# A layer norm's 1/std: a power on GpSimd, or a logarithm and an exponential on ScalarE

## The chip, the cores and the metric

The kernel runs on one core of a Trainium2 chip. A core has five engines with a queue each: TensorE (PE, matmuls; its weight loads are listed as PEld), VectorE (DVE), ScalarE (ACT), GpSimd (POOL) and SyncE (SP), which here issues the DMAs. Each engine works through its own queue in order and waits on semaphores for the others. The metric is the device time of one execution in microseconds.

## The reference

The input is 32 images of 128 channels and 56 x 56 pixels, in float32. Four layers follow one another, each of the form x = x + f(groupnorm(x)):

- layer 0: a 1x1 convolution with weights mixed by attention, then three dilated depthwise 3x3 convolutions with SiLU, summed
- layer 1: a cubic B-spline, the same for every element
- layer 2: linear attention over pooled cells, then a depthwise 3x3 convolution
- layer 3: a Mamba layer over the 3136 pixels as a sequence. It begins with a layer norm over the 128 channels of each pixel, and this is where the change lies:

```python
mu = jnp.mean(xs, axis=-1, keepdims=True)
var = jnp.mean(jnp.square(xs - mu), axis=-1, keepdims=True)
xn = (xs - mu) * lax.rsqrt(var + 1e-05) * norm_w + norm_b
...
delta = jax.nn.softplus(jnp.einsum('blr,dr->bld', dt, dt_proj_w) + dt_proj_b)
dA = jnp.exp(delta[..., None] * A)
...
h = dA_t * h + dBu_t
y = jnp.einsum('bdn,bn->bd', h, C_t)
```

The scan over pixels has 256 inner channels and 16 states each.

## The kernel before, in words

**Tiling.** The 128 channels lie on the 128 partitions. An image is cut into 7 chunks of 8 rows, that is 448 columns (`CH`). The 16 states of a chunk are handled two at a time for each half of the inner channels, in 16 steps (`STEPS`); so there are 32 x 7 = 224 chunks and 3584 steps.

**A step of the scan** (class `Scan`): ACT makes the decay exp(delta A) (`decay`, tile `da`, two instructions of 448 columns, in PSUM). DVE multiplies `du` by B into `h` and runs two scans over it (`state`); `h` has three buffers. POOL multiplies `h` by C into `hc`, which has two buffers (`products`). PE sums `hc` into `y` (`add`).

**The inputs of a chunk's scan** (`ssm_inputs`): matmuls from the normed `xn` give `xc`, `dbl` and the raw step sizes. The softplus is max(v,0) + ln(1 + exp(-|v|)): DVE takes the maximum into `delta`, ACT takes the absolute value, the exponential and the logarithm into `du`. POOL adds the two into `delta` and multiplies by `xc` into `du`; SP then moves both into the layout of the scan, with 16 DMAs a chunk. In the same stage the layer norm of the chunk after next is computed.

**The layer norm** (`layer_norm`, line 964): one matmul subtracts the channel mean (and applies the group norm) in PSUM, ACT takes the square and a copy `cen`, and a matmul with 1/128 gives the variance in PSUM. ACT then takes ln(var + eps) and exp(-0.5 times it) into `rstd`; POOL multiplies `cen` by `rstd` and applies weight and bias into `xn`. Ln and the kernel's other ACT functions (Exp, Tanh) are in different activation tables, so a Ln has an `ACT_TABLE_LOAD` ahead of it and another behind. For this the Ln of the softplus is passed in as `other` and kept together with the variance's Ln (lines 980 to 983). The first layer norm of an image is called from `until_scan` (line 1154), without `other`; after the last chunk (`norm is None`) only the softplus's Ln is left.

**The order of the work.** While one image is scanned, layers 1 and 2 of the next image (`until_scan`) and layer 0 of the one after (`first_layer`) are interleaved. In each group of images the instructions are collected by `Plan` with a price for each (`price`, line 163) and a due time that comes back from the work depending on it, and then put out in a planned order (`order`, `issue`, line 338, which is why nearly all instructions have line 338 in the profile). `together` keeps calls as one unit of this plan. On GpSimd the plan prices a two-input operation of over 8 columns at 0.14 + 0.00212 us a column, whatever it computes, and a power of up to 8 columns at 0.52 us. Six images make one turn of the loop (`UNROLL`), five turns, with two images ahead in the pipeline and two left over.

The group norms (`group_stats`, line 600) already take their 1/std, one column wide, by a power on GpSimd:

```python
nc.gpsimd.tensor_tensor(rs[:], ve[:], mhalf[:], ALU.pow)
```

`mhalf`, `one` and `lneps` (lines 446 to 448) are columns holding -0.5, 1 and 1e-5.

Of the kernel before, what the change touches and what calls it, by code (L numbers as in the profile page):

```python
# [14 lines left out]
AF = mybir.ActivationFunctionType  # L15
ALU = mybir.AluOpType
AX = mybir.AxisListType

P = 128
# [3 lines left out]
CH = ROWS * W  # L23
NCH = L // CH
# [338 lines left out]
def tile_conv_stack(ctx: ExitStack, tc: tile.TileContext, out: bass.AP, x: bass.AP, w: dict):  # L363
    nc = tc.nc
    B = x.shape[0]

    plan = Plan(nc, tc)
# [73 lines left out]
    def column(name, value):  # L441
        t = const.tile([P, 1], F32, name=name)
        nc.vector.memset(t[:], value)
        return t

    mhalf = column("mhalf", -0.5)
    one = column("one", 1.0)
    lneps = column("lneps", LN_EPS)
# [105 lines left out]
    xns = [const.tile([P, CH + DCONV - 1], F32, name=f"xn{k}") for k in range(3)]  # L554
# [6 lines left out]
    du = const.tile([P, DI, CH], F32, name="du")  # L561
# [18 lines left out]
    nc = plan  # L580

    def psum(cols=CH, rows=P):
        t = ps_mm.tile([P, 512], F32, tag="mm", name="mm")
        return t[:rows, :cols]
# [35 lines left out]
    def silu(dst, ps):  # L620

        t = tmp.tile([P, CH], F32, tag="v", name="t")
        nc.scalar.activation(t[:], ps, AF.Tanh)
        nc.vector.scalar_tensor_tensor(dst, t[:], 1.0, ps, ALU.add, ALU.mult)
# [332 lines left out]
    def norm_weights(st, ctr, cb):  # L957
# [3 lines left out]
        pm = psum(1)  # L961
        nc.tensor.matmul(pm, ctr[:], mg[:], start=True, stop=True)
        nc.vector.tensor_scalar_mul(cb[:], pm, -1.0)
    def layer_norm(xt, xn, j, norm, before=None, other=None):


        if norm is None:
            nc.scalar.activation(other, other, AF.Ln, bias=one[:, 0:1])
            return
        ctr, cb = norm  # L970
        pm = psum()
        nc.tensor.matmul(pm, ctr[:], xt[:, j * CH : (j + 1) * CH], start=True, stop=True)
        sq = tmp.tile([P, CH], F32, tag="v", name="sq")
        nc.scalar.activation(sq[:], pm, AF.Square, bias=cb[:, 0:1])
        cen = tmp.tile([P, CH], F32, tag="v", name="cen")
        nc.scalar.activation(cen[:], pm, AF.Identity, bias=cb[:, 0:1])
        pv = psum()
        nc.tensor.matmul(pv, jmat[:], sq[:], start=True, stop=True)
        rstd = tmp.tile([P, CH], F32, tag="v", name="rstd")
        with plan.together():  # L980
            nc.scalar.activation(rstd[:], pv, AF.Ln, bias=lneps[:, 0:1])
            if other is not None:
                nc.scalar.activation(other, other, AF.Ln, bias=one[:, 0:1])
        nc.scalar.activation(rstd[:], rstd[:], AF.Exp, scale=-0.5)
        nc.gpsimd.tensor_mul(rstd[:], cen[:], rstd[:])
        if before is None:
            nc.gpsimd.memset(xn[:, : DCONV - 1], 0.0)
        else:
            nc.gpsimd.tensor_copy(xn[:, : DCONV - 1], before[:, CH:])
        nc.gpsimd.tensor_scalar(xn[:, DCONV - 1 :], rstd[:], normw[:, 0:1], normb[:, 0:1], ALU.mult, ALU.add)  # L990
# [11 lines left out]
    def ssm_inputs(xt, k, norm):  # L1002

        dbl, xc = dbls[k % 2], xcs[k % 2]
        j, xn = k % NCH, xns[k % 3]
        for db in range(DI):
            ch = slice(db * P, (db + 1) * P)
            ps = psum()
            for i in range(DCONV):
                nc.tensor.matmul(ps, winT[:, i, ch], xn[:, i : i + CH], start=(i == 0), stop=False)  # L1010
            nc.tensor.matmul(ps, cbT[:, ch], onesr[:].to_broadcast([P, CH]), start=False, stop=True)
            silu(xc[:, db, :], ps)
            yield 3.3
        ps = psum()
        for db in range(DI):
            nc.tensor.matmul(ps, xprojT[:, db, :], xc[:, db, :], start=(db == 0), stop=(db == DI - 1))
        nc.scalar.copy(dbl[:], ps)
        nc.vector.scalar_tensor_tensor(dbl[:], dbl[:], low[:, 0:1], ps, ALU.mult, ALU.add)
        yield 1.7

        for db in range(DI):
            ps = psum()
            nc.tensor.matmul(ps, dtT[:, db * P : (db + 1) * P], dbl[:], start=True, stop=True)
            nc.scalar.activation(du[:, db, :], ps, AF.Abs, bias=dtb[:, db : db + 1])
            nc.vector.tensor_scalar(delta[:, db, :], ps, dtb[:, db : db + 1], 0.0, ALU.add, ALU.max)
            yield 0.8
        nc.scalar.activation(du[:], du[:], AF.Exp, scale=-1.0)
        layer_norm(xt, xns[(k + 1) % 3], j + 1, norm if j + 1 < NCH else None, xn, du[:])
        nc.gpsimd.tensor_add(delta[:], delta[:], du[:])
        nc.gpsimd.tensor_mul(du[:], delta[:], xc[:])  # L1030
        yield 4.0

        for db in range(DI):
            for src, dst in zip((delta, du), halves):
                dst = dst[DI * (k % 2) + db]
                for s in range(2):
                    for r in range(2):
                        nc.sync.dma_start(dst[Q * s : Q * s + Q, r, :], src[Q * r : Q * r + Q, db, :])
        yield 1.0
# [106 lines left out]
    def until_scan(b):  # L1146

        xt = xts[b % 3]
        st = yield from spline(xt, sts[b % 2])
        st = yield from linear_attention(xt, st)  # L1150
        norm = carried[b % 2]
        norm_weights(st, *norm)
        yield 5.0
        layer_norm(xt, xns[b * NCH % 3], 0, norm)
        yield 5.0

    def first_inputs(b):
        return ssm_inputs(xts[b % 3], b * NCH, carried[b % 2])
# [37 lines left out]
    def images(first, count, ahead):  # L1196
# [18 lines left out]
        for b in range(count):  # L1215
# [5 lines left out]
            for j in range(NCH):  # L1221
# [10 lines left out]
                if j + 1 < NCH:  # L1232
                    following = ssm_inputs(xt, k + 1, carried[b % 2])
                elif more:
                    following = first_inputs(b + 1)
# [153 lines left out]
```

## Time and profile before

| | |
|---|---|
| median of 3 runs | 16330.96 us (16321.42 to 16344.79) |
| profiled execution | 16316.11 us |
| its span | 16314.3 us, 212520 instructions |
| mean granted TensorE clock | 0.893 |
| each of 224 layer norms: logarithm, exponential | 634 ns and 568 ns |
| HBM traffic over the span | 59 GB/s |

The profile is of one execution. The span runs from the first to the last instruction. In a line for a group of instructions stand the line of code, the engine, the operation, the tile written and the tiles read, their shapes and the count; then the busy time in us and the mean of one in ns; then how long the engine had stood idle just ahead of these instructions, and what released it. In the table of waits a line reads: who waited, for whom, total us, times, longest us. In the order in time a line gives start, duration and, in brackets, the idle time ahead of it and its releaser.

### The profile page before, as it was taken

The numbers are of one execution on the slowest core, as the hardware profiler recorded it, in microseconds if no ns is written. First come the engines' busy times: TensorE is split into PE (matmuls) and PEld (weight loads), VectorE is DVE, ScalarE is ACT, GpSimd is POOL, SyncE is SP. The second block draws the span as 40 slices with busy tenths as digits, with TensorE's granted clock in tenths as the row PEclk, the third lists the DMA queues.
The fourth block names the chain that finished last, engine by engine and source line by source line (L and its number), as shares of the span: only waits on it lengthen the run. The fifth ranks groups of instructions, "written<-read, shape, count | busy, mean of one in ns | idle before, by whom it ended". The sixth has DMA issues, their size and how long they took to land. (4 is left out here: it accounts for less than half of the span.)

```text
span 16314.3 us, 212520 instructions
## 1 busy us (share of the span) xinstructions
PE 14202.3 (87%) x66400; PEld 4559.9 (28%) x66400; DVE 14306.2 (88%) x17314; ACT 11713.4 (72%) x21127; POOL 10785.0 (66%) x6406
## 2 busy tenths in 40 slices
PE   6888898888898888988888888888888898888887
PEld 2222222222222222222222222222222222222222
DVE  2898988989889898899988888888898898888889
ACT  3777777777677776777776777767777677776675
POOL 2676666666666666667666666666676666766666
PEclk7888998889998898998989988899988899888888
DMA  6344444344443444434444434444344444344421
GB/s 143 93 101 98 98 112 96 89 99 101 106 104 88 100 97 101 109 94 94 101 99 107 102 86 98 99 105 107 91 98 97 100 108 106 85 97 99 101 56 34
DMA packets 986159, 1589.93 MB, mean 97 GB/s; under 512 B 175622, under 2 KB 611209, under 8 KB 984331
## 3 DMA queue, kind: packets, MB, share of 16 engines
q1 hardware_dynamic: 985002, 1576.06, 41.0%
q8 instruction: 538, 8.81, 0.2%
q14 instruction: 619, 5.06, 0.1%
HBM read 785.62 MB, written 173.18 MB: 59 GB/s over the span
## 5 line engine op out<-in xcount | busy, mean ns | idle before, releaser
L338 POOL TENSOR_TENSOR hc<-h,cb 128x896 f32<-128x896 f32 x3584 | 7476.1, 2092 | 4173.5 <-DVE h L338 2178.7
L338 DVE TENSOR_TENSOR_SCAN h<-da,last,h 128x448 f32<-128x448 f32 x6144 | 6772.7, 1135 | 498.2 <-ACT da L338 451.3
L338 ACT ACTIVATE da<-delta,alog 128x448 f32<-128x448 f32 x7168 | 4481.8, 633 | 2635.3 <-DVE h L338 2369.4
L338 PE MATMUL y<-hc,sums 128*64 128x448 f32 x14336 | 3997.9, 638 | 625.6 <-POOL hc L338 617.8
L338 DVE TENSOR_TENSOR h<-du,pb 128x896 f32<-128x896 f32 x3584 | 3788.6, 1072 | 247.5 <-POOL hc L338 118.2
L338 PE MATMUL mm<-stack,dsT 96*32 96x448 f32 (+1 forms) x16128 | 1890.8, 575 | 59.4 <-DMA stack<-padded 16.8
L338 ACT ACTIVATE hats<-stack,bia,scl 128x448 f32<-128x448 f32 x2688 | 1887.6, 754 | 33.9 <-DVE bia L338 31.7
L338 PE MATMUL mm<-xn,winT 128*128 128x448 f32 x3584 | 1703.8, 590 | 39.8 <-ACT cb L338 13.5
L338 PEld LDWEIGHTS y<-hc,sums 128*64 128x64 f32 x14336 | 807.6, 147 | 2412.9 <-POOL hc L338 1436.9
L338 PE MATMUL mm<-hats,wspl 128*32 128x448 f32 x12544 | 1386.1, 563 | 33.3 <-ACT hats L338 30.4
L338 PE MATMUL pb<-dbl,sel 64*128 64x448 f32 x1792 | 918.3, 512 | 421.2 <-DVE h L338 364.3
L338 ACT ACTIVATE hats<-hats,one 128x1344 f32<-128x1344 f32 x896 | 1261.5, 1408 | 0.1
L338 ACT COPY cb<-mm 128x448 f32<-128x448 f32 x1792 | 940.3, 527 | 379.4 <-POOL hc L338 184.0
L338 PE MATMUL mm<-dbl,sel 64*128 64x448 f32 x1792 | 892.3, 502 | 363.5 <-DVE sz L338 63.7
L338 ACT ACTIVATE t<-mm 128x448 f32<-128x448 f32 x1568 | 829.2, 534 | 484.6 <-PE mm L338 480.3
L338 POOL TENSOR_TENSOR xt<-xt,g 128x448 f32<-128x448 f32 x672 | 767.5, 1142 | 524.1 <-DVE g L338 491.1
L338 DVE TENSOR_TENSOR_SCAN h<-da,h 128x448 f32<-128x448 f32 x1024 | 1054.1, 1070 | 28.3 <-ACT da L338 26.3
L338 PEld LDWEIGHTS mm<-xn,winT 128*128 128x128 f32 x3584 | 631.8, 197 | 986.0 <-issue 805.1
L338 DVE SCALAR_TENSOR_TENSOR g<-t,mm 128x448 f32<-128x448 f32 x672 | 407.7, 607 | 443.7 <-ACT t L338 392.8
L338 PEld LDWEIGHTS mm<-stack,dsT 96*32 96x32 f32 (+1 forms) x16128 | 445.2, 112 | 1156.3 <-issue 899.9
L338 PEld LDWEIGHTS mm<-dbl,sel 64*128 64x128 f32 x1792 | 351.2, 198 | 1453.5 <-issue 420.0
L338 PEld LDWEIGHTS pb<-dbl,sel 64*128 64x128 f32 x1792 | 358.6, 200 | 1419.1 <-issue 791.8
(187 smaller groups left out, 16166.2 us busy)
## 6 DMA issues: line engine op xcount, KB each, us to landing
stack<-padded SPq DMA_DIRECT2D x2688, 264.0 KB
stack<-xt SPq DMA_DIRECT2D x3584, 56.0 KB
delta<-delta SPq DMA_DIRECT2D x1792, 112.0 KB
du<-du SPq DMA_DIRECT2D x1792, 112.0 KB
padded<-yc SPq DMA_DIRECT2D x224, 264.0 KB
padded<-yc SPq DMA_DIRECT2D x256, 231.0 KB
xt<-x_dram SPq DMA_DIRECT2D x224, 224.0 KB
out_dram<-xt SPq DMA_DIRECT2D x224, 224.0 KB
```

Source lines behind the costliest of these rows:

```text
L338: call()
```

## The change

The variance plus eps is now copied out of PSUM by an ACT Identity with bias, and GpSimd raises it to the power -0.5, over 448 columns, with the column `mhalf` broadcast. The layer norm has no logarithm and no exponential any more. The softplus's logarithm is a call of its own in `ssm_inputs`, and the arguments that tied it to the layer norm are gone.

```diff
-    def layer_norm(xt, xn, j, norm, before=None, other=None):
-        if norm is None:
-            nc.scalar.activation(other, other, AF.Ln, bias=one[:, 0:1])
-            return
+    def layer_norm(xt, xn, j, norm, before=None):
         ctr, cb = norm
...
         rstd = tmp.tile([P, CH], F32, tag="v", name="rstd")
-        with plan.together():
-            nc.scalar.activation(rstd[:], pv, AF.Ln, bias=lneps[:, 0:1])
-            if other is not None:
-                nc.scalar.activation(other, other, AF.Ln, bias=one[:, 0:1])
-        nc.scalar.activation(rstd[:], rstd[:], AF.Exp, scale=-0.5)
+        nc.scalar.activation(rstd[:], pv, AF.Identity, bias=lneps[:, 0:1])
+        nc.gpsimd.tensor_tensor(rstd[:], rstd[:], mhalf[:].to_broadcast([P, CH]), ALU.pow)
         nc.gpsimd.tensor_mul(rstd[:], cen[:], rstd[:])
...
         nc.scalar.activation(du[:], du[:], AF.Exp, scale=-1.0)
-        layer_norm(xt, xns[(k + 1) % 3], j + 1, norm if j + 1 < NCH else None, xn, du[:])
+        nc.scalar.activation(du[:], du[:], AF.Ln, bias=one[:, 0:1])
+        if j + 1 < NCH:
+            layer_norm(xt, xns[(k + 1) % 3], j + 1, norm, xn)
         nc.gpsimd.tensor_add(delta[:], delta[:], du[:])
```

## The prediction

> **What bounds the kernel now.** I read the page's busy times first, then the groups of instructions around the scan and the layer norm, then the table of waits, then the order in time around one layer norm. The profiled execution took 16316.11 us, its span is 16314.3, and the median of the runs is 16330.96, 0.09% above. I do my sums on the span and add 15 us at the end, which is less than anything below depends on.
>
> The page's busy times:
>
> ```profile
> PE 14202.3 (87%) x66400; PEld 4559.9 (28%) x66400; DVE 14306.2 (88%) x17314; ACT 11713.4 (72%) x21127; POOL 10785.0 (66%) x6406
> ```
>
> There are 32 images of 7 chunks, so 224 chunks. Per chunk the span is 72.8 us, DVE is busy 63.9, PE 63.4, ACT 52.3 and POOL 48.1. DVE (with PE close to it) sets the pace; POOL has 24.7 us of idle time per chunk. The groups that matter, from the table of all groups:
>
> ```profile
> L338 POOL TENSOR_TENSOR hc<-h,cb 128x896 f32<-128x896 f32 x3584 | 7476.1, 2092 | 4173.5 <-DVE h L338 2178.7 <-PE y L338 1044.3 <-PE mm L338 227.2
> L338 DVE TENSOR_TENSOR_SCAN h<-da,last,h 128x448 f32<-128x448 f32 x6144 | 6772.7, 1135 | 498.2 <-ACT da L338 451.3
> L338 DVE TENSOR_TENSOR h<-du,pb 128x896 f32<-128x896 f32 x3584 | 3788.6, 1072 | 247.5 <-POOL hc L338 118.2 <-PE pb L338 88.7 <-DMA du<-du 20.8
> L338 ACT ACT_TABLE_LOAD x512 | 656.9, 1283 | 11.8 <-PE mm L338 3.9
> L338 POOL TENSOR_TENSOR rstd<-cen,rstd 128x448 f32<-128x448 f32 x224 | 255.0, 1138 | 36.8 <-ACT rstd L338 36.8
> L338 ACT ACTIVATE rstd<-mm,lneps 128x448 f32<-128x448 f32 x224 | 141.9, 634 | 5.4 <-PE mm L338 2.8
> L338 ACT ACTIVATE rstd<-rstd 128x448 f32<-128x448 f32 x224 | 127.3, 568 | 1.1
> L338 POOL TENSOR_TENSOR rs<-ve,mhalf 128x1 f32<-128x1 f32 x128 | 71.2, 556 | 169.8 <-DVE ve L338 168.7
> ```
>
> Each of the 16 steps of a chunk makes a state h on DVE (1.07 + 2 x 1.13 us) and multiplies it by C on POOL (2.09 us). The last line is the only power in the kernel: the 1/std of a group norm, one column wide, 0.556 us.
>
> DVE and POOL hold each other through the three buffers of h. From the table of waits:
>
> ```profile
> DVE h L338 <- ACT da L338: 478.9, 503, 3.0
> DVE h L338 <- POOL hc L338: 118.2, 93, 3.0
> ```
>
> Columns are total us, times, longest. DVE rarely waits for POOL, but the order in time (start, duration) shows how short the cover is. POOL, then DVE, around one layer norm:
>
> ```profile
> 8107.29 2.11 POOL L338 TENSOR_TENSOR hc<-h,cb 128x896 f32<-128x896 f32 x1
> 8109.46 2.10 POOL L338 TENSOR_TENSOR delta<-delta,du 128x896 f32<-128x896 f32 x1
> 8111.86 1.13 POOL L338 TENSOR_TENSOR rstd<-cen,rstd 128x448 f32<-128x448 f32 x1 [0.30 <-ACT rstd L338]
> 8113.10 0.71 POOL L338 TENSOR_SCALAR xn<-rstd,normw,normb 128x448 f32<-128x448 f32 x1
> 8113.78 2.10 POOL L338 TENSOR_TENSOR du<-delta,xc 128x896 f32<-128x896 f32 x1
> 8115.83 1.15 POOL L338 TENSOR_TENSOR xt<-xt,cube 128x448 f32<-128x448 f32 x1
> 8116.94 2.09 POOL L338 TENSOR_TENSOR hc<-h,cb 128x896 f32<-128x896 f32 x1
> ```
>
> ```profile
> 8113.92 2.18 DVE L338 TENSOR_TENSOR_SCAN h<-da,last,h 128x448 f32<-128x448 f32 x2
> 8119.06 1.09 DVE L338 TENSOR_TENSOR h<-du,pb 128x896 f32<-128x896 f32 x1 [2.96 <-POOL hc L338]
> ```
>
> POOL leaves its hc products at 8109.4 and comes back at 8116.9. DVE runs dry at 8116.1, 6.7 us after POOL left, and stands until the next hc has ended at 8119.0. So whatever POOL does in one piece beyond some 5 us is paid by DVE nearly one for one; the 24.7 us of idle POOL time are no cover for a long single instruction.
>
> [...] The trace shows the 1283, but no drain (the load of 8106.52 is followed by the logarithm at 8107.82), so I use 1.283 us a load. [...] (2092 - 1138)/448 = 2.13 ns a column, with 184 ns fixed. [...]
>
> **The change, part by part.**
>
> *Taken from ACT.* 224 exponentials at 0.568 = 127 us. The logarithm of the variance becomes an Identity with the same bias column and 448 columns: the like row (cen, Identity from PSUM with a bias column) has 627 ns against 634, so nothing. The softplus keeps its Ln in each chunk, so its two table loads stay: 2 x 224 = 448 of the 512. The other 64 are two for each image's first layer norm, whose Ln stands alone (loads at 15861.92 and 15863.87 around it); they go: 64 x 1.283 = 82 us. ACT loses 209 us, 0.93 a chunk. ACT is 72% busy and most of its own idle time is for DVE's h, so I count this at nothing in the likeliest case: DVE's waits for POOL will cover it. Without that cover, all of it on the path, it would be 209 us.
>
> *Order.* The two logarithms were one unit, so the softplus's Ln waited for the variance's matmul and now does not. POOL's delta and du, and the four-fold DMAs of each on SP, depend on it; SP already waits 1967 us in total for delta. A gain here of a microsecond in some chunks is lost under the next part.
>
> *Added to POOL.* 224 powers of 448 columns, C us each. This is the unknown. The one-column power costs 556 ns where a two-input operation of one column would be 186: 370 ns [...]. The ends: if all 370 ns are a fixed cost, C = 1.14 + 0.37 = 1.5 us. If every column pays it anew, C = 0.19 + 448 x 0.372 = 167 us. [...] These are estimates. I take the overlapped loop, C = 17 us.
>
> *What C costs.* Queued behind the power on POOL are its own multiply, xn, often delta and du, and then the hc that frees h for DVE and feeds PE's y. In the row shown DVE would stand C longer. Where the power stands apart from delta and du, the 6.7 us of supply minus the 2.09 of the next hc and the 1.85 of multiply and xn leave 2.8 us. I take half, 1.4, and add 2.6 of DVE's 8.9 idle us a chunk, waits for ACT and PE that get ahead during the hole: 4 us hidden. So 17 - 4 = 13 us a chunk, 224 x 13 = 2912, and 16314 + 2912 = 19226; with the 15 us, 19240. POOL's floor, 48.1 + 17 = 65.1 a chunk, does not bind. The DMAs of delta and du, and SP's loads behind them, go late by C too, but the next chunk's states stand behind the same POOL queue, so they aren't charged again. PE's hole may lower its clock (0.78 in the first 430 us where it is less busy, 0.90 later); 63.4 x 0.9/0.78 = 73 still fits in 86.
>
> The power also reads two SBUF inputs. [...] the small vv of the group norms averages 611 ns on one column. States and scans read one of their inputs from PSUM, so this touches four small chains an image, mostly in holes.
>
> **The rivals.**
>
> 1. *The pow loop takes its columns overlapped, 14 to 21 us* (above): 16314 + 224 x (14 - 7) = 17900 to 16314 + 224 x 21 = 21000, around 19240.
> 2. *Shorter, 3 to 14 us.* For it: is_ge with a multiply on 448 columns takes 1867 ns where multiply with add takes 716, so POOL's odd operations can be only a few times dearer. [...] 16400 to 18500.
> 3. *Few columns in flight, 21 to 70 us.* At C = 42, 16314 + 224 x 38 = 24830. At 70, 31100.
> 4. *One column after the other, up to 167 us.* [...] POOL becomes the bound: floor (48.1 + 167) x 224 = 48200, with DVE's stand 16314 + 224 x 163 = 52800. At C = 118, 41900.
> 5. *Faster.* The 370 ns are a fixed cost and C = 1.5 lies in POOL's idle 24.7 us; the 82 us of table loads and POOL's 36.8 us of waiting for ACT's rstd come off the path: 16331 - 119 = 16210, -0.7%. It decides below C of about 1.3 us if each of the 93 waits for hc grows by C (93 x 1.3 = 121), and up to perhaps 2 if the planner finds it room. [...]
>
> **How the numbers follow.** Chances: case 1 35%, case 2 17%, case 3 19%, case 4 19%, case 5 with its neighbours (C under 3) 10%, of which 6 faster, 4 within 0.2%. A measurement of this kernel can tell about 0.2% (33 us) from no change. Faster 0.06, same 0.04, slower 0.90. The predicted time is case 1's 19240, whose own range is 17900 to 21000. The 8-in-10 range runs from 16300, which leaves out the faster 6, to 42000, which leaves out C above 118, about 10.
>
> **What would show it.** The group of the new power on POOL gives C directly; the wait of DVE's h for POOL's hc should grow from 118 us to about 224 x 13, with POOL's busy time up by 224 C. ACT should show 448 table loads and 127 us less in Exp. The prediction is wrong if C is under 5 us, where the waits hardly move, or near 100, where POOL's busy share goes above 90%; its step from C to time is wrong if the span grows by clearly less than C - 7 a chunk.

## The result and the profile after

The changed kernel takes 32176.25 us (median of 4 runs, 32175.21 to 32178.51) against 16327.31 us (median of 4 runs of the kernel before): 1.9698 times the time before, with a 95% interval of 1.967 to 1.9726. The profiled execution took 32178.51 us, its span is 32176.7. The prediction was 19240; the direction was right and the size was not: 15849 us were added, where it had 2912.

The page's busy times after the change:

```profile
PE 14763.4 (46%) x66400; PEld 4703.5 (15%) x66400; DVE 14407.4 (45%) x17314; ACT 11583.6 (36%) x20844; POOL 26835.0 (83%) x6630
```

POOL has 16050 us more work, DVE and ACT about what they had, PE 4% more, and the span has grown by 15862. The groups that answer to those of before:

```profile
L338 POOL TENSOR_TENSOR rstd<-rstd,mhalf 128x448 f32<-128x448 f32 x224 | 16070.2, 71742 | 315.4 <-ACT rstd L338 313.9 <-ACT last L338 1.6
L338 DVE TENSOR_TENSOR h<-du,pb 128x896 f32<-128x896 f32 x3584 | 3796.1, 1073 | 4495.4 <-POOL hc L338 4311.4 <-PE pb L338 101.3 <-DMA du<-du 33.6
L338 ACT ACT_TABLE_LOAD x453 | 581.2, 1283 | 85.2 <-PEq L1279 59.4 <-DMA out_dram<-xt 13.9 <-DMA delta<-delta 5.7
L338 POOL TENSOR_TENSOR rs<-ve,mhalf 128x1 f32<-128x1 f32 x128 | 71.9, 561 | 131.6 <-DVE ve L338 131.6
```

One power over 448 columns takes 71.74 us, as long as a whole chunk took before (72.8). 224 of them are 16070 us, 1.3% more than all that was lost. The table loads fell from 512 (before, two around each of 256 places with a logarithm: 224 of the softplus and 32 first layer norms) to 453, as foreseen (448), and the exponentials are gone.

What DVE waits for, from the table of waits (total us, times, longest):

```profile
DVE h L338 <- POOL hc L338: 4311.4, 174, 68.1
DVE cube L338 <- POOL rstd L338: 4171.1, 61, 70.9
DVE g L338 <- POOL rstd L338: 3565.9, 50, 71.9
```

The first is the wait that the prediction named. The two others, nearly twice as large together, it did not name: `cube` and `g` are written into the five shared `v` tiles, and one of these is held by `cen` until the multiply behind the power has read it. In the order in time both look the same. POOL, then DVE:

```profile
15967.53 2.11 POOL L338 TENSOR_TENSOR hc<-h,cb 128x896 f32<-128x896 f32 x1 [0.21 <-DVE h L338]
15974.07 71.74 POOL L338 TENSOR_TENSOR rstd<-rstd,mhalf 128x448 f32<-128x448 f32 x1 [4.44 <-ACT rstd L338]
16045.89 1.13 POOL L338 TENSOR_TENSOR rstd<-cen,rstd 128x448 f32<-128x448 f32 x1
```

```profile
15974.09 1.06 DVE L338 TENSOR_TENSOR h<-du,pb 128x896 f32<-128x896 f32 x1
16047.05 0.62 DVE L338 SCALAR_TENSOR_TENSOR g<-t,mm 128x448 f32<-128x448 f32 x1 [71.89 <-POOL rstd L338]
```

Here DVE does one more instruction and then stands for the whole power. On average over the 224 powers DVE is busy for 4.84 us of the 71.74, PE for 4.72 and ACT for 6.04 (busy time of each engine summed over the stretches of the powers).

### The profile page after: what moved, and what is told of

Its sections match the earlier page's. It is cut to its first block, busy times and chain, and to the rows that moved or that the text cites. A ratio compares the mean times of both kernels' runs of the same rounds, so it can differ in the third digit from the quotient of the medians.

```text
span 32176.7 us, 213061 instructions
## 1 busy us (share of the span) xinstructions
PE 14763.4 (46%) x66400; PEld 4703.5 (15%) x66400; DVE 14407.4 (45%) x17314; ACT 11583.6 (36%) x20844; POOL 26835.0 (83%) x6630
## 5 line engine op out<-in xcount | busy, mean ns | idle before, releaser
L338 POOL TENSOR_TENSOR rstd<-rstd,mhalf 128x448 f32<-128x448 f32 x224 | 16070.2, 71742 | 315.4 <-ACT rstd L338 313.9
L338 PE MATMUL y<-hc,sums 128*64 128x448 f32 x14336 | 4188.1, 665 | 8759.6 <-POOL hc L338 8754.6
L338 DVE TENSOR_TENSOR cube<-sq,mm 128x448 f32<-128x448 f32 x448 | 271.8, 608 | 4285.8 <-POOL rstd L338 4171.1
L338 PE MATMUL mm<-xt,aggT 128*128 128x448 f32 x448 | 299.6, 763 | 4052.2 <-DVE cube L338 2031.2
L338 PE MATMUL mm<-stack,dsT 96*32 96x448 f32 (+1 forms) x16128 | 1984.9, 597 | 55.2 <-DMA stack<-onesd 17.8
L338 PE MATMUL mm<-xn,wzT 128*128 128x448 f32 x896 | 657.8, 829 | 2648.6 <-DVE g L338 2183.4
L338 ACT ACTIVATE sq<-mm 128x448 f32<-128x448 f32 x448 | 237.4, 532 | 4238.6 <-POOL xt L338 2084.0
```

The lines of the kernel that those rows point to most:

```text
L338: call()
```

## The experiments

Three theories. A: all of the loss is POOL's time in the power, and almost none of it is hidden. B: only the duration was mis-sized, and the prediction's step from duration to time (4 us hidden) holds. C: the rest of the change, the order and the two logarithms apart, has a share. "Hidden" below is the duration of the power less the time that it added per chunk, counted from the run with the power left out (16325.9 us). A time without an interval is that of one execution.

One thing bears on all of them. An edit that changes an instruction's price changes the whole planned order. The multiply below has the power's price in the plan, and its trace has the power's order: POOL and ACT take their instructions in the same sequence throughout. With the power left out, or with fewer columns, some 2000 of POOL's 6406 other instructions stand at another place in the sequence. So the multiply is the clean comparison for what the power itself costs; differences of one or two per cent between runs with other orders can come from the order as well.

**The power replaced by a multiply.**

```diff
-nc.gpsimd.tensor_tensor(rstd[:], rstd[:], mhalf[:].to_broadcast([P, CH]), ALU.pow)
+nc.gpsimd.tensor_tensor(rstd[:], rstd[:], mhalf[:].to_broadcast([P, CH]), ALU.mult)
```

> The changed kernel with the power replaced by a multiply of the same shape in the same place (the 1/std is left out, so the values are not the reference's). Theory A (all of the loss is the time that the power occupies POOL): the multiply takes 1.14 us in place of 71.74, and the time is 16300 us within 1%. The ACT work taken away is then worth at most 209 us, and I expect about 60 of it less what 224 x 1.14 us on POOL cost: 16250 to 16400. Theory C (the order of the work, with the two logarithms apart, costs a part of it): the time stays above 16700.

Measured: 16487.85 us, 1.0093 times the kernel before (1.0077 to 1.0108). The group:

```profile
L338 POOL TENSOR_TENSOR rstd<-rstd,mhalf 128x448 f32<-128x448 f32 x224 | 209.9, 937 | 299.3 <-ACT rstd L338 298.8 <-ACT last L338 0.2
```

It missed the range that I gave (16250 to 16400) by 88 us, but theory C's 16700 is not reached: 99% of the loss is the power's own. In the same order an instruction longer by 70.80 us costs 70.04 us a chunk. Still, a version with a nearly free instruction in the power's place is slower than before.

**The power left out.** The line is deleted; the 1/std is not computed.

> The changed kernel with the power left out and nothing in its place (the 1/std is not computed). Against the run with a multiply in its place (+0.93%) this tells what the extra POOL instruction costs. If that instruction's 0.94 us is the cause: 224 x 0.94 = 210 us less, 16280 us, near before or a little below. If the new order is the cause (DVE waits 146 + 130 us in linear attention for PE that it didn't before): still near 16480.

Measured: 16325.9 us, 0.9997 (0.9987 to 1.0007). Taking ACT's exponentials and 59 table loads away is worth nothing, in this order of the work. The version with the multiply takes 162 us more, 0.72 a chunk for 0.94 us on POOL. That this is POOL's time is not shown, because the order differs too. DVE's waits in linear attention, with the multiply and then without it:

```profile
DVE kb L338 <- PE mm L338: 145.7, 32, 5.9
DVE ws L338 <- PE mm L338: 129.8, 32, 4.6
```

```profile
DVE kb L338 <- PE mm L338: 15.8, 9, 4.5
DVE ws L338 <- PE mm L338: 13.7, 12, 4.6
```

With the multiply these two are 246 us longer, while DVE waits for POOL's `hc` less (83 against 145 us). This points to the order, and the changed kernel has the same two waits (272 us).

**The logarithm and the exponential back, the two logarithms apart.**

```diff
-nc.scalar.activation(rstd[:], pv, AF.Identity, bias=lneps[:, 0:1])
-nc.gpsimd.tensor_tensor(rstd[:], rstd[:], mhalf[:].to_broadcast([P, CH]), ALU.pow)
+nc.scalar.activation(rstd[:], pv, AF.Ln, bias=lneps[:, 0:1])
+nc.scalar.activation(rstd[:], rstd[:], AF.Exp, scale=-0.5)
```

> The changed kernel with the logarithm and the exponential put back on ScalarE, so that of the change only the separation of the two logarithms is left. Up to 224 more pairs of table loads, 2.57 us each: 575 us more on ACT. If ACT's time is free (the run with the power left out took 209 us from it and gained nothing): within 0.3% of before. If it is on the path in this direction: up to 3.5% slower.

Measured: 16621.46 us, 1.0175 (1.0159 to 1.019).

```profile
L338 ACT ACT_TABLE_LOAD x671 | 860.9, 1283 | 104.0 <-PEq L1279 66.6 <-DMA out_dram<-xt 15.5 <-PE mm L338 6.4
```

671 loads are 159 more than before, 204 us, and the time is up by about 280. Against the run with the power left out, ACT is busy 352 us longer and the time is up by 296. So work added to ACT was not free, where what was taken away bought nothing; how much of this is the order, these runs don't separate. In the changed kernel this cost does not arise, since no second logarithm is left to be apart from.

**The power over a quarter and over an eighth of the columns.**

```diff
-nc.gpsimd.tensor_tensor(rstd[:], rstd[:], mhalf[:].to_broadcast([P, CH]), ALU.pow)
+nc.gpsimd.tensor_tensor(rstd[:, :CH // 4], rstd[:, :CH // 4], mhalf[:].to_broadcast([P, CH // 4]), ALU.pow)
```

> The changed kernel with the power over the first 112 of 448 columns only (three quarters of the 1/std are left out). By the two durations seen, 0.556 us for 1 column and 71.74 for 448, the power takes 18.2 us, near the 17 that the prediction was made for. Theory A (nothing or nearly nothing of a power is hidden, about 0.9 us as in the changed kernel): 16314 + 224 x 17.3 = 20190 us. Theory B (the prediction's step from duration to time holds, 4 us are hidden): 16314 + 224 x 14.2 = 19495 us.

> The changed kernel with the power over 56 of 448 columns only (seven eighths of the 1/std are left out). The power takes 9.3 us by the same straight line. Theory A (0.9 us hidden): 16314 + 224 x 8.4 = 18196 us. Theory B (4 us hidden): 16314 + 224 x 5.3 = 17501 us. If the loss after the power comes from TensorE's clock falling during a long hole, a hole this short should lose less than A says and lie nearer to B.

Measured: 19998.89 and 18186.01 us. The groups of the quarter and of the eighth:

```profile
L338 POOL TENSOR_TENSOR rstd<-rstd,mhalf 128x112 f32<-128x112 f32 x224 | 4081.3, 18220 | 85.1 <-ACT rstd L338 82.7 <-ACT last L338 1.6
```

```profile
L338 POOL TENSOR_TENSOR rstd<-rstd,mhalf 128x56 f32<-128x56 f32 x224 | 2078.3, 9278 | 149.7 <-ACT rstd L338 148.8 <-ACT last L338 0.8
```

The durations lie near a straight line: (71.742 - 9.278)/392 = 0.1593 us a column, with 0.36 to 0.40 us fixed. The quarter is the prediction's C (18.2 for 17) and tests its second step alone:

| power | duration us | added per chunk us | hidden us |
|---|---|---|---|
| multiply in its place | 0.94 | 0.72 | 0.21 |
| 56 columns | 9.28 | 8.30 | 0.98 |
| 112 columns | 18.22 | 16.40 | 1.82 |
| 448 columns | 71.74 | 70.76 | 0.98 |

Theory A, for every length of the power; B's 4 us are not there. The eighth hides no more than the whole, so there is no sign that a short hole escapes what pays the cover back. The differences among these hidden times, under 1 us a chunk, are no larger than what another order can make (246 us in linear attention are 1.1 a chunk), so nothing is read from them, nor from the multiply's row.

**Tiles of their own for `cen` and `rstd`.**

```diff
-cen = tmp.tile([P, CH], F32, tag="v", name="cen")
+cen = tmp.tile([P, CH], F32, tag="cen", name="cen", bufs=1)
...
-rstd = tmp.tile([P, CH], F32, tag="v", name="rstd")
+rstd = tmp.tile([P, CH], F32, tag="rstd", name="rstd", bufs=1)
```

> The changed kernel with cen and rstd in tiles of their own instead of two of the five shared v tiles. In the changed kernel about half of DVE's long stands end at the layer norm's multiply (cube and g waiting for POOL's rstd: 4171 + 3566 us, 111 times), because a v tile is held by cen until the power is over. Theory A1 (the v tiles cut the cover short): DVE's work inside the power grows from 4.84 us towards the 6.7 seen before, and the time falls by up to 224 x 1.9 = 420 us, to 31750. Theory A2 (whatever is done inside the hole is paid back after it, by the backlog on POOL and TensorE's low clock): 32000 to 32300.

Measured: 32222.62 us, 0.1% above the changed kernel. DVE's waits for `rstd` are gone, and the largest of its waits is now for `hc`:

```profile
DVE h L338 <- POOL hc L338: 10317.3, 270, 70.7
```

DVE is busy for 6.91 us of each power instead of 4.84, close to the 6.7 us of supply that the prediction had read from the trace. The time did not move: A2. What DVE gains inside the hole it loses outside.

**The plan told the true price.**

```diff
-w.cost += 0.14 + n * (1.2e-3 if not slow else 2.12e-3 if method != "tensor_scalar" else 3.8e-3)
+if ALU.pow in args:
+    w.cost += 0.4 + 0.1592 * n
+else:
+    w.cost += 0.14 + n * (1.2e-3 if not slow else 2.12e-3 if method != "tensor_scalar" else 3.8e-3)
```

> The changed kernel with only the plan's price of the power put right (0.4 + 0.1592 us a column, 71.7 in place of 1.09), so that the order of all engines is planned around it. If the order is what costs beyond POOL's busy time: down towards POOL's floor, (48.1 + 71.7) x 224 = 26840 us. If the buffers are what holds DVE (three of h, two of hc): the order can't help, 31500 to 32300.

Measured: 31690.3 us, 1.5% below the changed kernel and inside the range of the second case: the order helps, by little. 3.15 us of a power are now hidden, and DVE does 8.34 us of work inside it.

**The power in eight pieces of 56 columns**, with the true price.

```diff
-nc.gpsimd.tensor_tensor(rstd[:], rstd[:], mhalf[:].to_broadcast([P, CH]), ALU.pow)
+for q in range(8):
+    part = slice(q * (CH // 8), (q + 1) * (CH // 8))
+    nc.gpsimd.tensor_tensor(rstd[:, part], rstd[:, part], mhalf[:].to_broadcast([P, CH // 8]), ALU.pow)
```

> The changed kernel with the power cut into eight instructions of 56 columns, and the plan told their true price (0.4 + 0.1592 us a column) so that it can put other POOL work between them. A piece takes 9.28 us, the eight 74.2. Theory A (nearly nothing of a hole is hidden, 0.9 us each): 16314 + 224 x 8 x 8.4 = 31370 us. Theory D (a short hole with hc products between hides DVE's supply of some 4.6 us, and what is paid back stands only behind the last piece, before the multiply and xn): POOL becomes the bound, (48.1 + 74.2) x 224 = 27400 us and up to 28500.

Measured: 31416.99 us, theory A's number, but not a fair test: the plan mostly put the pieces in rows. The 224 powers lie in 333 rows, 202 of them with seven or more pieces. A row of eight, in the order in time on POOL:

```profile
16027.70 73.85 POOL L341 TENSOR_TENSOR rstd<-rstd,mhalf 128x56 f32<-128x56 f32 x8
16101.51 4.11 POOL L341 TENSOR_TENSOR hc<-h,cb 128x896 f32<-128x896 f32 x2
```

**The same pieces, each due 60 us later in the plan**, so that `hc` goes ahead of them.

```diff
+for w in self.works:
+    if w.engine == "gpsimd" and w.cost > 5.0:
+        w.due += 60.0
```

> The kernel with the power in eight pieces, but each piece given a due time 60 us later in the plan, so that hc products go ahead of it whenever they are ready; before, the eight often stood in one row of 73.9 us. Theory A (each hole is paid in full but for 0.9 us): 31000 to 31500. Theory D (DVE works some 4.6 us inside each hole and POOL becomes the bound): 27400 to 28500.

Measured: 29887.25 us, between the two theories. The pieces now lie in 889 rows, 664 of them of one piece:

```profile
16094.90 9.27 POOL L345 TENSOR_TENSOR rstd<-rstd,mhalf 128x56 f32<-128x56 f32 x1 [0.20 <-ACT rstd L345]
16104.14 2.07 POOL L345 TENSOR_TENSOR hc<-h,cb 128x896 f32<-128x896 f32 x1
```

Hidden are 13.6 us a chunk, against 6.8 with the pieces in longer rows and 3.15 in one instruction, all three with the true price. Per row this is 13.6 x 224/889 = 3.4 and 6.8 x 224/333 = 4.6 us: with an order planned for it, a hole hides three to five microseconds on average, in one row a chunk as in four.

**Matmuls of no use during the power.** The granted TensorE clock, averaged over stretches after every second power, is 0.50 in the first 5 us, 0.59 in the next and over 0.85 only from 30 us on (before the change, behind the same multiply: 0.88 and 0.79). PE is nearly as loaded as DVE (87% and 88% of the span before), so this could be what pays the cover back.

```diff
+first = small.tile([P, 1], F32, tag="first", name="first")
+nc.scalar.copy(first[:], rstd[:, 0:1])
+pw = psum()
+with plan.together(1000):
+    for _ in range(120):
+        nc.tensor.matmul(pw, jmat[:], first[:].to_broadcast([P, CH]), start=True, stop=True)
 nc.gpsimd.tensor_tensor(rstd[:], rstd[:], mhalf[:].to_broadcast([P, CH]), ALU.pow)
```

> The changed kernel with 120 matmuls of no use on PE, released when the Identity ahead of the power is done, some 65 us at full clock, so that TensorE does not stand during the power. The granted clock in the 10 us after a power was 0.50 and 0.59; here it should be near 0.9. If the low clock is what pays back DVE's cover after the hole: up to 224 x 4 = 900 us less, 31300. If it is POOL's backlog (the multiply, xn and the first hc, 3.9 us, before DVE gets its first h): 32000 to 32400, or more where these matmuls hold up others behind them.

> The last run's 120 useless matmuls took 0.76 us each with their weight loads, 91 us, and outlasted the power by 20. Here 88 of them, 67 us, end just before it. If TensorE's low clock after the hole (0.50 and 0.59 in the first 10 us of the changed kernel) pays the cover back: the clock stays near 0.9 and the time falls by up to 900 us, to 31300. If it isn't the clock: 32000 to 32500.

Measured: 36975.72 us with 120 and 33106.83 us with 88. The first expectation's 65 us answer to 120 times the 539 ns (median) that the layer norm's matmul with `jmat` takes before. Neither gained. With 88 the clock was 0.82 in the first 5 us and 0.61 in the next, so it did not stay near 0.9, and these matmuls held up PE's own work. DVE's wait for `pb`, 101 us in total in the changed kernel, became:

```profile
DVE h L338 <- PE pb L338: 5490.6, 189, 68.4
```

DVE's work in the first 5 us after a power hardly changed: 2.15 us, against 2.02 in the changed kernel. With so much of PE taken this doesn't decide whether the clock pays the cover back; it only shows no gain to be had in this way.

**The same function with a narrow power.** The variance is the same on all 128 partitions, so 448 values are raised 128 times each. Four matmuls put them into 112 partitions x 4 columns, and four more with the identity spread the result.

```diff
+part = CH // 4
...
+for c in range(4):
+    nc.tensor.matmul(pv[:, c : c + 1], sq[:, c * part : (c + 1) * part], jmat[:, 0:1], start=True, stop=True)
...
+nc.scalar.activation(vr[:], pv, AF.Identity, bias=lneps[:part, 0:1])
+nc.gpsimd.tensor_tensor(vr[:], vr[:], mhalf[:part, :].to_broadcast([part, 4]), ALU.pow)
...
+for c in range(4):
+    nc.tensor.matmul(pr[:, c * part : (c + 1) * part], vr[:, c : c + 1].to_broadcast([part, P]), ident[:part, :part], start=True, stop=True)
...
+nc.scalar.copy(rstd[:], pr)
```

> The same function with the power over 112 partitions x 4 columns: the variance is the same on all partitions, so four small matmuls put it into columns, and four more with the identity spread the result again; an ACT copy brings it to SBUF. The power should take 0.40 + 4 x 0.16 = 1.04 us. ACT loses the exponential and 64 table loads and gains 0.2 + 0 us, PE gains some 1.7 us a chunk. Theory A: the loss is gone, 16250 to 16700 us; above before if PE's added work counts in full (224 x 1.7 = 380), below it if ACT's 209 us do.

Measured: 16675.4 us, 1.0209 (1.0195 to 1.0223).

```profile
L338 POOL TENSOR_TENSOR vr<-vr,mhalf 112x4 f32<-112x4 f32 x224 | 229.3, 1024 | 191.7 <-ACT vr L338 190.5
```

About half the time of the changed kernel, for the same 1/std, by giving the power 4 columns instead of 448. It does not reach the kernel before: the time is 335 us above it, with PE busy 625 us longer and another order. No run separates these two.

**The change turned round: POOL's work given to ACT, and to DVE.** From the kernel before, `xn`'s weight and bias on ACT; then also the spline's `ind` on DVE.

```diff
-nc.gpsimd.tensor_scalar(xn[:, DCONV - 1 :], rstd[:], normw[:, 0:1], normb[:, 0:1], ALU.mult, ALU.add)
+nc.scalar.activation(xn[:, DCONV - 1 :], rstd[:], AF.Identity, bias=normb[:, 0:1], scale=normw[:, 0:1])
...
-nc.gpsimd.tensor_scalar(ind[:], xs, top[:, 0:1], clast, ALU.is_ge, ALU.mult)
+nc.vector.tensor_scalar(ind[:], xs, top[:, 0:1], clast, ALU.is_ge, ALU.mult)
```

> The kernel before with the layer norm's weight and bias (xn, 0.716 us on POOL) applied by an ACT Identity with scale and bias instead. It turns the change's direction round: 160 us from POOL to ACT. If POOL's time is on the path at 0.7 us for 1, as the multiply run showed, and ACT's is free: 16340 - 0.7 x 160 = 16225 us, 0.7% faster. If both are free: no change.

> The last one with the spline's indicator (ind, 1.87 us on POOL in each chunk) on DVE besides. POOL loses 418 us more and DVE gains some 0.6 us x 224 = 134 us. If POOL's time costs 0.7 for 1 and DVE's 1 for 1: a further 160 us less, 16070 us. If only DVE's counts: 134 us more than the last.

Measured: 16407.84 us, 1.0041 (1.0027 to 1.0055), and 16897.14 us, 1.0338 (1.0324 to 1.0352). Both expectations of a gain fell. In the first POOL had 155 us less to do and ACT 162 more, and the time rose by 67. In the second DVE took 0.945 us for `ind`, not 0.6, and the time rose by another 489 us, over twice DVE's added 211; its waits for PE and ACT grew as well. The work moved off POOL was not free where it went, and no gain came of POOL's relief; what part the new orders have in this is not separated. No version in this study beats the kernel before.

## Why the prediction was wrong, point by point

**What bounds the kernel**: right as far as it went. DVE and PE stand with POOL in one chain, and with 24.7 us of idle POOL time a chunk, 1.0 us of an instruction of 71.74 was hidden.

**The duration, "I take the overlapped loop, C = 17 us"**: this is the step that failed. The power takes 71.74 us, 4.2 times that. Its bounds, 1.5 and 167 us, held (the time of 32176 us lies in the prediction's wide range as well), and the measured value falls between the rivals of a few columns in flight (to 70) and one column after the other. The one-column instruction had misled in both directions: of its 0.556 us, about 0.40 is fixed by the line through the other widths, of which an ordinary operation has 0.19, so the power's extra of 0.37 was some 0.21 of fixed cost and 0.16 of column, and each further column costs that 0.16 again. The prediction's 14, 17, 21 and 42 us were the author's estimates from an assumption about how the columns of a power overlap, with nothing in the trace for it; 17 us over 448 columns is 0.04 us a column, where the line gives 0.16. Why a column takes 0.16 us is not shown by any run.

**From duration to time, "4 us hidden"**: this step failed too, by less. With the true C it gives 16314 + 224 x 67.7 = 31480, 2.2% under what was measured; at the quarter's 18.2 us 19495, where 19999 was measured. It erred on the side that the prediction's own sign (a growth of clearly less than C - 7 a chunk) did not watch. The runs show 1.0 to 1.8 us hidden in all. That is about the size of its first term, the 1.4 us from the buffers, but they don't show that it is the same thing: DVE does 4.84 us of work in the hole and most of that is lost again. Its second term, 2.6 us that DVE was to win back from its other idle time, failed. DVE's idle time outside the powers went up instead: (143.6 - 71.7) - (64.3 - 4.8) = 12.4 us a chunk after, 9.0 before.

**Why so little stays hidden.** That an order planned for a power of 1.09 us is part of it is shown: with the true price 3.15 us are hidden, and pieces with `hc` between them hide 13.6 a chunk. That the `v` tiles are not it is shown as well: without them DVE works 6.9 us in the hole, near the predicted 6.7, and the time stays. Of the two ways in which the rest may be paid back, TensorE's low clock and POOL's backlog of multiply, `xn` and the first `hc`, the traces point to the second. Against the multiply, which has the same order, DVE's idle time outside the powers grew by 3.1 us a chunk: idle time that ended with POOL grew by 2.7 us, with PE by 0.7, and with ACT it fell by 0.3. In the first 5 us after a power POOL is busy for 4.86 and PE for 2.08. No run changed the backlog alone, so as a cause this stays open.

**ACT's 209 us at nothing**: right in its effect, 0.9997 with the power left out (ACT's busy time fell by 147 us there). The rival of a faster kernel fell twice over: the power was not cheap, and with a power at no cost there was still no gain.

**The waits**: h for `hc` was to grow to 2912 us and grew to 4311. By the prediction's own rule and the true duration it would have been 224 x 67.7 = 15165, so it is luck that the two lie so near each other: this wait has a far smaller share of a far larger loss. The `v` tiles, through which another 7737 us are waited, were missed: I had followed who reads the result of the stalled instruction, not who needs the tiles that its inputs keep.

**The two SBUF inputs**: that the power would hold up small DVE instructions with two SBUF inputs was the author's estimate. It did not: the 20 `vv` that began inside a power took at most 0.22 us. The 611 ns that the prediction read for `vv` go with POOL's `hc`: before, the 35 of 128 that began during an `hc` took 1.71 us on average, and 68 beside an idle POOL 0.20. States and scans were not held up by it before: the 985 `h` from `du` and `pb` that lay wholly inside an `hc` took 1.08 us on average, 315 beside an idle POOL 1.08, and the scans `h` from `da`, `last` and `h` 1.14 and 1.13.

## What to carry to other kernels

The price of this power could not be read from a one-column instance: measure an unknown operation at two widths before giving it a wide tile, and give it as few columns as the data has different values. Time added to one queue of a chain like this was paid by about nine tenths at 9 and 18 us and by 99% at 72, while time taken off ACT, busy for 72% of the span before, bought nothing (0.9997); idle time on a page was no measure of cover (with POOL idle for 24.7 us a chunk, 1.0 us of a power's 71.74 was hidden). Where an order is planned from prices, a wrong price is a cost beside the instruction itself (1.5% here), and two versions are compared cleanly only where the order is the same.

## What the runs showed of the hardware

- A power on GpSimd: 0.56 us for 1 column, 1.02 for 4 (on 112 partitions), 9.28 for 56, 18.22 for 112, 71.74 for 448. The same two operands multiplied take 0.94 us at 448 columns, and 1.14 where neither is a broadcast column.
- The power does not keep DVE from reading two SBUF inputs. POOL and DVE in the order in time of the changed kernel:

```profile
8576.35 71.74 POOL L338 TENSOR_TENSOR rstd<-rstd,mhalf 128x448 f32<-128x448 f32 x1
```

```profile
8578.73 0.13 DVE L338 TENSOR_TENSOR dm<-mv,mg 128x1 f32<-128x1 f32 x1
8579.77 0.21 DVE L338 SCALAR_TENSOR_TENSOR vv<-dm,mv 128x1 f32<-128x1 f32 x1
```

Both read two SBUF tiles 2.4 and 3.4 us into the power and are not held up (0.13 and 0.21 us). So it is with all 20 `dm` and all 20 `vv` that began inside a power: none took over 0.14 and 0.22 us.

- POOL's multiply `hc` does hold them up. A `vv` that began 0.33 us into an `hc` ended with it, in the changed kernel:

```profile
16308.59 2.09 POOL L338 TENSOR_TENSOR hc<-h,cb 128x896 f32<-128x896 f32 x1 [2.31 <-DVE dm L338]
16308.92 1.77 DVE L338 SCALAR_TENSOR_TENSOR vv<-dm,mv 128x1 f32<-128x1 f32 x1
```

The 55 `vv` that began during an `hc` took 1.57 us on average, those beside an idle POOL 0.20. Why `hc` holds them up and the power does not is not shown.

- TensorE's granted clock was 0.53 over the whole power at 15974.07 and 0.62 in the 10 us after it, with 1.00 in the 10 us before and in the next 10 after. Averaged over the powers it was 0.50 in the first 5 us behind one and over 0.85 only from 30 us on.
